# Attention scores of a window one step sooner, in the second halves of their PSUM banks

## The chip, the cores and the metric

The kernel runs on one core of a Trainium2 chip. The metric is the device time of one execution in microseconds (us); the time shown is the median of three runs. A core has five queues of instructions that run beside each other and wait for each other by semaphores: TensorE (PE in the profile), VectorE (DVE), ScalarE (ACT), GpSimd (POOL) and SyncE (SP), which here issues all DMAs.

## The reference

A network of two layers on 16 images of 128 channels by 56 by 56 pixels, in float32. The change lies in the first layer, a block with routed window attention. An image is cut into 7 by 7 = 49 windows of 8 by 8 pixels. For each window the four windows whose mean keys fit its mean query best are selected, and each of its 64 pixels attends, in 4 heads of 32 channels, to the 4 * 64 = 256 pixels of the selected windows:

```python
x = x + _dwconv(x, pos_w, pos_b)
y = _ln(xh, ln1_g, ln1_b)
qkv = y @ qkv_w + qkv_b
logits = jnp.einsum('bpc,bqc->bpq', q_win * SCALE, k_win)
_, idx = jax.lax.top_k(logits, TOPK)
kv_sel = jax.vmap(lambda t, i: t[i])(kv_pix, idx)
...
att = jnp.einsum('bpqhd,bpkhd->bphqk', q_pix * SCALE, k_sel)
att = jax.nn.softmax(att, axis=-1)
o = jnp.einsum('bphqk,bpkhd->bpqhd', att, v_sel)
...
o = (o + lepe) @ wo_w + wo_b          # lepe: 5x5 depthwise convolution of the values
xh = xh + o
z = gelu(_ln(xh) @ mlp_w1 + mlp_b1) @ mlp_w2 + mlp_b2
```

The second layer (a 3x3 convolution, a scan over sequences of 8 tokens and a group norm) isn't touched.

## The kernel before

`layer0` works on the images one after the other. For each there are 49 steps (`step(im, nxt, t)`, t is the window) and then the feed-forward part `mlp(im, nxt)`, which also ends the work on the last row of windows. Beside the attention of image `im`, the steps carry the first normalisation and projections of the next image `nxt`, the output projection and second normalisation of the row of windows before, the 5x5 convolution tap by tap on VectorE (`convolve_on`), and the 3x3 position convolution of later images on POOL (`beside_to`).

The order within each engine is the program's own: `_chain` ties every instruction to the one before it on its engine, so no scheduler moves anything. What waits for what between engines is found by the Tile framework from the tiles that instructions read and write. Buffers of a tile name turn over in pools of 1, 2, 3 or 6.

One window t passes through these stages:

- `gather` (L393): four DMAs on SP bring the selected windows' keys and values into `sel` (six buffers). Step t issues the gather of window t + 5; the first five are issued in the MLP of the image before. SP also loads an image's pixels in steps 20 and 24 (`load`, L288), and stores the results of the MLP.
- `scores` (L410): four matmuls of TensorE (eight instructions in the profile) write the scores of two heads into the first 256 columns of bank 0 of the PSUM tile `ps`, and of the other two into those of bank 1. `ps` has one buffer of two banks of 512 columns; the second halves stay unused.
- `largest` (L420): VectorE takes the maximum over the 256 scores, of both banks in one instruction, into the statistics tile `sst` (three buffers).
- `exponentials` (L424): ScalarE, once for each bank, with the negative maximum as bias and the sum as a second output, into the tiles `e` (three buffers).
- `inverse` (L432): VectorE takes the reciprocal of the sums; `weights` (L436): POOL multiplies.
- In step t + 1 TensorE transposes the weights into `ptt` and ScalarE copies them to `att`; in step t + 2 `attend` (L468) multiplies by the values. The values of `sel` are transposed into `pvt` for two windows at once (L446).

`open_step` is scores and maximum together. In step t they are those of window t; those of window 0 stand near the end of the MLP of the image before. The MLP's first hidden block (L549) uses bank 0 of `ps` too.

Of the kernel before, what the change touches and what calls it, by code (L numbers as in the profile page):

```python
# [12 lines left out]
AF = mybir.ActivationFunctionType  # L13
ALU = mybir.AluOpType
AX = mybir.AxisListType
# [6 lines left out]
NW = WIN * WIN  # L22
# [187 lines left out]
def layer0(ctx: ExitStack, tc: tile.TileContext, x, t, x1, conv):  # L210
# [11 lines left out]
    nc = tc.nc  # L222
# [35 lines left out]
    ps = banks.tile([P, 2, 512], F32, tag="ps", name="ps")  # L258


    bias = cst.tile([P, 6], F32, tag="bias", name="bias")
    for i in range(6):
        w, b = (wqkv[:, i, :], ln1_b) if i < 3 else (wm1[:, i - 3, :], ln2_b)
# [24 lines left out]
    def load(b, two):  # L288
        nc.sync.dma_start(pads[b % 2][64 * two : 64 * two + 64, 1 : H + 1, 1 : W + 1], xv[b, two])
# [33 lines left out]
    def squared(n):  # L323
        sq = held["sq"] = w1.tile([P, BLK], F32, tag="sq", name=f"sq_{n}")
        nc.scalar.activation(sq, held["pc"], AF.Square)
# [5 lines left out]
    def deviation(n):  # L331
        rstd = held["rstd"] = w1.tile([P, BLK], F32, tag="rstd", name=f"rstd_{n}")
        nc.scalar.activation(rstd, held["pv"], AF.Ln, bias=eps)
        nc.scalar.activation(rstd, rstd, AF.Exp, scale=-0.5)
# [3 lines left out]
    def windows(im, i):  # L338

        n = f"{im['b']}_{i}"  # L340
        y = held["y"] = w1.tile([P, BLK], F32, tag="y1", name=f"y1_{n}")
        nc.vector.tensor_mul(
            y.rearrange("c (w r x) -> c w r x", w=WIN, r=8),
            held["pc"].rearrange(by_row, r=8, w=WIN),
            held["rstd"].rearrange(by_row, r=8, w=WIN),
        )
        if i == 0:
            im["sum"] = w2.tile([P, NW], F32, tag="ysum", name=f"ysum_{n}")
            im["kv"] = w2.tile([P, NW, WP, 2], F32, tag="kv", name=f"kv_{n}")
        nc.vector.tensor_reduce(  # L350
            im["sum"][:, WIN * i : WIN * i + WIN], y.rearrange("c (w p) -> c w p", p=WP), AX.X, ALU.add
        )
# [5 lines left out]
    def keep(im, i, s):  # L358
        src = held["pq", s].rearrange("c (w p) -> c w p", p=WP)
        if s == 0:  # L360
            q = im["q"][i] = w1.tile([P, WIN, WP], F32, tag=f"q{i}", name=f"q_{im['b']}_{i}")
            nc.scalar.activation(q, src, AF.Identity, bias=bias[:, 0:1], scale=SCALE)
        else:
            kv = im["kv"][:, WIN * i : WIN * i + WIN, :, s - 1]
            nc.scalar.activation(kv, src, AF.Identity, bias=bias[:, s : s + 1])
# [27 lines left out]
    def gather(im, w):  # L393
        sel = im["sel", w] = w6.tile([P, TOPK, WP, 2], F32, tag="sel", name=f"sel_{im['b']}_{w}")
        if w % 2 == 0:
            n = min(2, NW - w)
            _, im["at"] = nc.values_load_multi_w_load_instructions(
                im["line"][:, w : w + n, :].rearrange("o w j -> o (w j)"), engines=(mybir.EngineType.SP,),
                min_val=0, max_val=NW - 1, skip_runtime_bounds_check_because="the indices are at most 48",
            )  # L400
        vs = im["at"][TOPK * (w % 2) :]
        for j in range(TOPK):
            nc.sync.dma_start(
                sel[:, j, :, :].rearrange("c p s -> c (p s)"),
                im["kv"][:, bass.ds(vs[j], 1), :, :].rearrange("c o p s -> c (o p s)"),
            )

    def scores(im, w):  # L410

        q, sel = im["q"][w // WIN][:, w % WIN, :], im["sel", w]
        for h in range(HEADS):
            p, s = divmod(h, 2)
            rows = slice(HD * h, HD * h + HD)
            nc.tensor.matmul(  # L416
                ps[64 * s : 64 * s + 64, p, 0:256], lhsT=q[rows], rhs=sel[rows, :, :, 0].rearrange("c j p -> c (j p)"), start=True, stop=True
            )

    def largest(im, w):  # L420
        st = im["st", w] = w3.tile([P, 3, 2], F32, tag="sst", name=f"sst_{im['b']}_{w}")
        nc.vector.tensor_reduce(st[:, 0, :], ps[:, :, 0:256], AX.X, ALU.max, negate=True)  # L422

    def exponentials(im, w):  # L424
        st = im["st", w]
        im["e", w] = [w3.tile([P, 256], F32, tag=f"e{p}", name=f"e{p}_{im['b']}_{w}") for p in range(2)]
        for p, e in enumerate(im["e", w]):
            nc.scalar.activation(  # L428
                e, ps[:, p, 0:256], AF.Exp, bias=st[:, 0, p : p + 1], accum_out=st[:, 1, p : p + 1]
            )  # L430

    def inverse(im, w):  # L432
# [35 lines left out]
    def attend(im, w):  # L468

        at, v = im["att", w], im["v", w]  # L470
        out = po[:, (w % WIN) * WP : (w % WIN + 1) * WP]
        for h in range(2):
            for head in range(HEADS):
                p, s = divmod(head, 2)
                rows = slice(HD * head, HD * head + HD)
                nc.tensor.matmul(
                    out[rows], lhsT=v[:, h, rows], rhs=at[:, p, h, s * WP : (s + 1) * WP],
                    start=(h == 0), stop=(h == 1), skip_group_check=True,
                )
# [41 lines left out]
    def collect(im, r):  # L521
        o = held["o"] = w1.tile([P, BLK], F32, tag="o", name=f"o_{im['b']}_{r}")
        nc.vector.tensor_add(
            o.rearrange("c (r w x) -> c r w x", r=8, w=WIN),
            po[:, 0:BLK].rearrange("c (w r x) -> c r w x", w=WIN, r=8),
            im["lepe", r].rearrange("c (r w x) -> c r w x", r=8, w=WIN),
        )
# [5 lines left out]
    def residual(im, r):  # L533
        xh = im["xh"][r]
        nc.vector.scalar_tensor_tensor(xh, held["pw"], wo_b, xh, ALU.add, ALU.add)

    def second(im, r):
        y2 = im["y2"][r] = w1.tile([P, BLK], F32, tag=f"y2{r}", name=f"y2_{im['b']}_{r}")
        nc.vector.tensor_mul(y2, held["pc"], held["rstd"])
# [49 lines left out]
    def open_step(im, t):  # L589
        scores(im, t)  # L590
        largest(im, t)

    def step(im, nxt, t):
        r, c = divmod(t, WIN)
        b = im["b"]
        n = f"{b}_{t}"
        out, row = (im, r - 1) if r else (images[b - 1], NBLK - 1)
        old, new = r > 0 or b > 0, nxt is not None
        if t + AHEAD < NW:
            gather(im, t + AHEAD)  # L600
        if t == 0 and early and not new:
            conv.load(0)
        if t in (20, 24) and b + 2 < NB:
            load(b + 2, t // 4 - 5)

        if c < 3 and new and r:
            keep(nxt, r - 1, c)
        if c == 2 and old:
            residual(out, row)
        if c == 3 and old:  # L610
            squared(n)
        if c == 4 and old:
            deviation(n)
        if c == 5 and new:
            squared(n)
        if c == 6 and new:
            deviation(n)
        if t > 0 or b == 0:
            open_step(im, t)
        if t > 1:  # L620
            attend(im, t - 2)
        if c == 1 and r:
            collect(im, r - 1)
        if c == 4 and old:
            second(out, row)
        if c == 6 and new:
            windows(nxt, r)
        convolve_on(TAPS[c] - 1)
        if new:
            if t == 1:  # L630
                position(nxt, 1, (8,))
            if t in ENDS:
                position(nxt, 2 + ENDS.index(t), (8,))
            if t < 45:
                beside_to(b + 1, LEAD + -(-(ROUND - LEAD) * (t + 1) // 45))
            else:
                beside_to(b + 2, 3 * (t - 44) // 2)
        exponentials(im, t)
        inverse(im, t)
        if t in (1, 8, 17, 27):  # L640
            surround(im, 3 + (1, 8, 17, 27).index(t))
        if t in (36, 44) and new:
            surround(nxt, (t - 36) // 8)
        weights(im, t)
        if c == 1 and new and r:
            project(g0, 2)
        waits = c in (1, 4, 6)
        if not waits:
            piece(im, nxt, out, row, c, r)
        if t > 0:  # L650
            transpose_weights(im, t - 1)
            keep_weights(im, t - 1)
        if c % 2 == 0:
            transpose_values(im, t)
            keep_values(im, t)
        convolve_on(1)
        if waits:
            piece(im, nxt, out, row, c, r)
# [83 lines left out]
    start = len(nc.cur_bb.bb.instructions)  # L742
    _act_set(tc, EXP_LN)
    im = images[0]
# [49 lines left out]
    for b in range(NB):  # L794
        im, nxt = images[b], images[b + 1] if b + 1 < NB else None
# [575 lines left out]
```

## Time and profile before

| | |
|---|---|
| median of three runs | 8305.27 us (8295.65 to 8312.71) |
| the profiled execution | 8300.8 us, its span 8299.0 us |
| mean granted clock of TensorE | 0.984 |
| TensorE, VectorE, ScalarE, POOL busy | 94%, 92%, 69%, 85% of the span |
| first layer | to about 3150 us of the span |
| one image in the first layer | about 188 us, of them 146 us from the scores of window 1 to those of window 48 |

How to read the profile's lines. A group's line gives source line, engine, operation, output <- inputs, shapes and count; then the busy time in us and the mean of one instruction in ns; then how long the engine was idle just before these instructions, and who ended most of that. A line of a timeline gives the start in us, the length, the engine and the operation; in square brackets how long the engine had been idle before, and for whom. `SPq` is SP's queue; for it the length covers all issues of the line, with the waits between them. PEld is the loading of weights into TensorE, which runs beside its matmuls.

### The profile page before, as it was taken

To read this page: it belongs to the slowest core of one execution; us is meant where nothing else is said; L and a number is where in the kernel's file an instruction comes from. 1 tells how busy PE (TensorE), PEld (TensorE's weight loads), DVE (VectorE), ACT (ScalarE), POOL (GpSimd) and SP (SyncE) were. 2 spreads that over 40 slices of the span, in tenths; PEclk is the share of its full clock that TensorE was granted. 3 is DMA by queue.
4 is the path that set the end of the run, shared out by engine and by line. 5 is a ranking of instruction groups with operands and counts; after the bars stand their busy time and mean duration, and the time that the engine had idled before them with its cause. 6 is when DMAs were issued, how large, how long until landed. Compare 5 with 4: busy or idle time off the path is not lost.

```text
span 8299.0 us, 151691 instructions
## 1 busy us (share of the span) xinstructions
PE 7837.1 (94%) x53308; PEld 3375.2 (41%) x53308; DVE 7631.6 (92%) x10124; ACT 5685.7 (69%) x10691; POOL 7030.7 (85%) x5584
## 2 busy tenths in 40 slices
PE   6999999999999998999999999999999999999998
PEld 3444444444444453333333333333333333333333
DVE  8999999999999976999999999999999999999998
ACT  4777777777777755666666666766666666666665
POOL 7888888888888725899989989999989989989997
PEclk8999999999999998999999999999999999999998
DMA  3333333333333223333333334334334334334333
GB/s 72 87 86 85 82 89 87 87 87 89 90 88 87 74 79 83 87 93 98 101 94 99 97 91 105 92 96 105 85 102 107 86 101 103 89 98 106 90 91 85
DMA packets 765478, 757.89 MB, mean 91 GB/s; under 512 B 189616, under 2 KB 664880, under 8 KB 762800
## 3 DMA queue, kind: packets, MB, share of 16 engines
q1 hardware_dynamic: 764720, 748.19, 35.3%
q8 instruction: 426, 6.98, 0.4%
q14 instruction: 332, 2.72, 0.1%
HBM read 439.61 MB, written 102.76 MB: 65 GB/s over the span
## 4 chain that ended last, share of the span: by engine, by line
PE 52%; DVE 21%; POOL 11%; ACT 10%; issue 5%; DMA 0%; SPq 0%; ACTq 0%; DVEq 0%; POOLq 0%
PE a L997 11%; PE pq L185 9%; PE pq L1043 6%; POOL xh L317 5%; PE x L1008 4%; DVE lepe L519 4%; PE pq L917 4%; DVE h L1015 3%; POOL tap L315 3%; PE pq L1077 3%; DVE sst L422 2%; PE pq L956 2%; PE pq L1049 2%; ACT e L428 2%; DVE a L1025 2%
## 5 line engine op out<-in xcount | busy, mean ns | idle before, releaser
L1034 POOL TENSOR_TENSOR cst<-h,cb 128x1792 f32<-128x1792 f32 x784 | 3129.5, 3998 | 342.6 <-DVE h L1030 273.1
L1000 ACT ACTIVATE a<-a 128x896 f32<-128x896 f32 x1568 | 1415.8, 903 | 1191.7 <-PE x L1008 961.0
L1015 DVE TENSOR_TENSOR h<-x,bb 128x896 f32<-128x896 f32 x1568 | 1698.2, 1083 | 134.1 <-PE x L1008 100.5
L519 DVE SCALAR_TENSOR_TENSOR lepe<-vpad,lep,lepe 128x448 f32<-128x448 f32 x2688 | 1717.8, 678 | 0.5
L1008 PE MATMUL x<-dtx,amask 32*128 32x448 f32 x6272 | 1620.9, 593 | 42.1 <-DVE h L1015 32.5
L997 PE MATMUL a<-dt,adec 32*128 32x448 f32 x6272 | 1616.3, 591 | 38.6 <-DVE h L1030 36.8
L1025 DVE TENSOR_TENSOR a<-a,h 128x896 f32<-128x896 f32 x1344 | 1466.1, 1091 | 69.3 <-ACT a L1000 64.9
L1030 DVE TENSOR_TENSOR h<-a,h 128x896 f32<-128x896 f32 x1344 | 1465.8, 1091 | 42.0
L438 POOL TENSOR_SCALAR e<-e,sst,zero 128x256 f32<-128x256 f32 x1568 | 855.3, 555 | 566.9 <-DVE sst L434 514.0
L428 ACT ACTIVATE e<-ps,sst 128x256 f32<-128x256 f32 x1568 | 727.0, 469 | 541.2 <-DVE sst L422 492.1
L997 PEld LDWEIGHTS a<-dt,adec 32*128 32x128 f32 x6272 | 472.8, 184 | 1037.9 <-issue 295.1
L317 POOL TENSOR_TENSOR xh<-xh,tap 128x448 f32<-128x448 f32 x749 | 859.4, 1147 | 33.9
L185 PE MATMUL pq<-pad,conv 128*128 128x448 f32 x1890 | 834.7, 559 | 0.0
L1043 PE MATMUL pq<-cst,sel 128*32 128x448 f32 x6272 | 731.3, 551 | 0.0
L422 DVE TENSOR_REDUCE sst<-ps 128x2 f32<-128x512 f32 x784 | 540.5, 689 | 99.6 <-PE ps L416 76.9
L146 ACT ACT_TABLE_LOAD x484 | 621.0, 1283 | 9.5 <-PEq L1362 0.7
L416 PE MATMUL ps<-sel,q 32*64 32x256 f32 x6272 | 541.1, 414 | 55.7 <-ACT e L428 45.9
L460 PE MATMUL ptt<-ident,e 128*128 128x128 f32 x3136 | 521.5, 282 | 73.4 <-POOL e L438 64.5
L1008 PEld LDWEIGHTS x<-dtx,amask 32*128 32x128 f32 x6272 | 473.7, 184 | 266.7 <-DVE h L1015 243.2
L460 PEld LDWEIGHTS ptt<-ident,e 128*128 128x128 f32 x3136 | 371.0, 142 | 373.4 <-issue 185.5
L466 ACT COPY att<-ptt 128x512 f32<-128x512 f32 x784 | 457.8, 584 | 64.8 <-PE ptt L460 54.9
L185 PEld LDWEIGHTS pq<-pad,conv 128*128 128x128 f32 x1890 | 324.2, 189 | 357.9 <-issue 350.2
(182 smaller groups left out, 12453.2 us busy)
## 6 DMA issues: line engine op xcount, KB each, us to landing
sel<-kv SPq DMA_DIRECT2D x3136, 64.0 KB
bb<-db SPq DMA_DIRECT2D x336, 448.0 KB
cb<-dc SPq DMA_DIRECT2D x336, 448.0 KB
x<-r SPq DMA_DIRECT2D x112, 224.0 KB
pad<-x SPq DMA_DIRECT2D x16, 1568.0 KB
db<-bs SPq DMA_DIRECT2D x112, 224.0 KB
dc<-cs SPq DMA_DIRECT2D x112, 224.0 KB
bb<-db SPq DMA_DIRECT2D x112, 224.0 KB
```

Source lines behind the costliest of these rows:

```text
L185: self.nc.tensor.matmul(bank[:, 0:BLK], lhsT=self.weights[:, k, :], rhs=self.pad[:, 8 * i + dy : 8 * i + dy + 8, dx : dx + W], start=(k == ...
L317: nc.gpsimd.tensor_add(im["xh"][i], im["xh"][i], held["tap"])
L428: nc.scalar.activation(e, ps[:, p, 0:256], AF.Exp, bias=st[:, 0, p : p + 1], accum_out=st[:, 1, p : p + 1])
L519: nc.vector.scalar_tensor_tensor(out, src, lep[:, k : k + 1], acc, ALU.mult, ALU.add)
L997: nc.tensor.matmul(a[:, k, :], lhsT=adec[rows, l4, :], rhs=p["dt"][rows, h, :], start=True, stop=True)
L1000: nc.scalar.activation(p["a", l, jp], p["a", l, jp], AF.Exp)
L1008: nc.tensor.matmul(x[:, k, :], lhsT=mask[rows, l4, :], rhs=p["dtx"][rows, h, :], start=True, stop=True)
L1015: nc.vector.tensor_mul(p["h", l][:, own(jp), :], px["x"], weight)
L1025: nc.vector.tensor_mul(a, a, before)
L1030: nc.vector.tensor_add(h, p["a", l, jp], h)
L1034: nc.gpsimd.tensor_mul(c, p["h", l], p["gate", 1, l].unsqueeze(1).to_broadcast([P, 4, BLK]))
L1043: nc.tensor.matmul(py[32 * j : 32 * j + 32], lhsT=sel[:, l4, :], rhs=p["c", l][:, j, :], start=False, stop=(l % 4 == 3), skip_group_check= ...
```

## The change

Scores, maximum and exponentials of odd windows use columns 256 to 511 of the two banks, those of even windows columns 0 to 255. Step t issues scores and maximum of window t + 1 in the place where those of window t stood. Step 0 of the first image issues those of window 0 as well; in later images these stay in the MLP. Step 48 issues none. Exponentials, reciprocal, weighting and all that comes later keep their steps.

```diff
+    def half(w):
+        return slice(256 * (w % 2), 256 * (w % 2) + 256)
+
     def scores(im, w):
...
             nc.tensor.matmul(
-                ps[64 * s : 64 * s + 64, p, 0:256], lhsT=q[rows], rhs=sel[rows, :, :, 0].rearrange("c j p -> c (j p)"), start=True, stop=True
+                ps[64 * s : 64 * s + 64, p, half(w)], lhsT=q[rows], rhs=sel[rows, :, :, 0].rearrange("c j p -> c (j p)"), start=True, stop=True
             )
 
     def largest(im, w):
...
-        nc.vector.tensor_reduce(st[:, 0, :], ps[:, :, 0:256], AX.X, ALU.max, negate=True)
+        nc.vector.tensor_reduce(st[:, 0, :], ps[:, :, half(w)], AX.X, ALU.max, negate=True)
 
     def exponentials(im, w):
...
             nc.scalar.activation(
-                e, ps[:, p, 0:256], AF.Exp, bias=st[:, 0, p : p + 1], accum_out=st[:, 1, p : p + 1]
+                e, ps[:, p, half(w)], AF.Exp, bias=st[:, 0, p : p + 1], accum_out=st[:, 1, p : p + 1]
             )
...
-        if t > 0 or b == 0:
+        if t == 0 and b == 0:
             open_step(im, t)
+        if t + 1 < NW:
+            open_step(im, t + 1)
         if t > 1:
             attend(im, t - 2)
```

## The prediction

> **What bounds the kernel now.** The change touches the attention steps of the first layer alone, so I read the page for the shares, then the view of the score tile `ps` (who waits for it), then the timeline of one image's start and of the SP queue.
>
> ```profile
> PE 7837.1 (94%) x53308; PEld 3375.2 (41%) x53308; DVE 7631.6 (92%) x10124; ACT 5685.7 (69%) x10691; POOL 7030.7 (85%) x5584
> L428 ACT ACTIVATE e<-ps,sst 128x256 f32<-128x256 f32 x1568 | 727.0, 469 | 541.2 <-DVE sst L422 492.1
> L422 DVE TENSOR_REDUCE sst<-ps 128x2 f32<-128x512 f32 x784 | 540.5, 689 | 99.6 <-PE ps L416 76.9
> L416 PE MATMUL ps<-sel,q 32*64 32x256 f32 x6272 | 541.1, 414 | 55.7 <-ACT e L428 45.9
> ```
>
> TensorE and VectorE are both full to over nine tenths. The 492.1 us that ScalarE waits for the maximum look like the prize, but ScalarE is 69% busy and costs nothing by waiting. What the engines that set the pace lose around the scores is small: TensorE 45.9 us before L416 until an exponential has left the banks; VectorE 76.9 us before the maximum, and (view of `ps`) 60.5 us before the reciprocal L434.
>
> The second resource is SP's queue, which isn't in the busy shares. Each step gathers one window's selection with four DMAs:
>
> ```profile
> 1244.73 62.54 SPq L403 DMA_DIRECT2D sel<-kv  x84
> 1307.37 0.68 SPq L289 DMA_DIRECT2D pad<-x  x1
> 1308.82 14.32 SPq L403 DMA_DIRECT2D sel<-kv  x16
> 1323.18 0.66 SPq L289 DMA_DIRECT2D pad<-x  x1
> 1324.60 60.81 SPq L403 DMA_DIRECT2D sel<-kv  x76
> ```
>
> ```profile
> 1724.17 0.68 PE L416 MATMUL ps<-sel,q 32*64 32x256 f32 x8 [0.53 <-DMA sel<-kv]
> ...
> 590.69 0.36 PE L446 MATMUL pvt<-ident,sel 128*128 128x128 f32 x1 [0.53 <-DMA sel<-kv]
> ```
>
> 84 issues in 62.54 us are 2.98 us for a gather, waits included; a step takes 3.06 us (scores at 1261.50 and, seven steps on, 1282.91). SP is nearly full. The two image loads in steps 20 and 24 (L289) throw it back: the 16 issues between them took 14.32 us, 3.58 a gather. After them SP can't catch up. The second fence, from the timelines of two other images, shows TensorE already waiting for a gather, in scores and in transposes.
>
> How near it is follows from the trace's records of each gather's landing (updates of its semaphore), set against the starts of the scores. In the image that begins at 1432 us:
>
> ```
> window  last issue ends  landed   scores of it   scores one step sooner
> 24      1495.23          1496.55  1504.66        1501.83
> 30      1520.08          1523.87  1524.01        1520.39
> 33      1529.55          1532.28  1533.45        1529.48
> 48      1575.65          1578.64  1578.86        1576.25
> ```
>
> Up to window 25 a selection lies there 5 to 8 us before it is wanted even one step sooner. From 26 on it comes about when the step before takes its scores, or after. At window 30 it landed 0.14 us ahead of its use, and 3.48 us behind the place that the scores are to be moved to.
>
> **The change part by part.** (1) Other halves. Same matmuls, reduction and exponentials, same sizes; no row changes. Cost nil.
>
> (2) In step t TensorE now does scores t+1, VectorE maximum t+1, both in the places where those of t stood; steps 1 to 47 keep the order of all engines but for the index. What ScalarE waits for decides. The exponentials of t follow maximum t+1 in program order and read the same two banks. In the changed program as built, the wait of e(t) on VectorE's semaphore is for the count that maximum t+1 gives (in the old one, maximum t), and the scores of t+1 still wait for e(t-1). So the halves are not treated as separate: in every step scores, maximum and exponentials follow each other in the same places. The row for what that chain costs is 45.9 us (L416 on ACT e). By addresses alone, e(t) needs only its own maximum, a step old, and up to 45.9 us would go. The Trainium skill (PSUM — Partial Sum Buffer, section on bank collisions) says that two engines on one bank and the same partitions collide even at different columns, so guard by bank and not by address; by that rule the gain is 0. No run here shows a collision, but the built wait is the rule's. I take 0. The 492.1 us wait stays, as do the 60.5 and 76.9.
>
> (3) Start of an image. Before, maximum 0 stands in the MLP, and step 0 has neither scores nor maximum:
>
> ```profile
> 1242.92 0.68 DVE L422 TENSOR_REDUCE sst<-ps 128x2 f32<-128x512 f32 x1
> 1243.52 0.67 DVE L557 SCALAR_TENSOR_TENSOR r<-po,vec,xh 128x448 f32<-128x448 f32 x1
> 1243.69 0.47 ACT L428 ACTIVATE e<-ps,sst 128x256 f32<-128x256 f32 x1 [4.11 <-DVE sst L422]
> 1244.11 1.86 DVE L519 SCALAR_TENSOR_TENSOR lepe<-vpad,lep,lepe 128x448 f32<-128x448 f32 x3
> ...
> 1245.88 0.15 DVE L434 RECIPROCAL sst<-sst 128x2 f32<-128x2 f32 x1
> ...
> 1246.75 0.98 PE L460 MATMUL ptt<-ident,e 128*128 128x128 f32 x4 [1.30 <-POOL e L438]
> ```
>
> Now scores 1 come first; they wait for maximum 0 (ends 1243.60) and start at about 1243.72. Maximum 1 can start 0.82 us after (as at 1274.10 and 1274.92, where it waited), 1244.54, instead of the taps at 1244.19: 0.35 us of wait and 0.69 of work. Exponential 0 slips to 1245.3 to 1246.2, which the three taps (1.77) cover. Reciprocal 0 goes from 1245.88 to 1246.95; POOL, idle there, weights 1.07 later; TensorE, idle for POOL, transposes 1.07 later; after that it has no gap to make it good, and maximum and scores of the next steps follow. So about 1.07 us later per image. In step 48 scores and maximum are gone (0.68 and 0.69 us), but nothing gains: TensorE then waits for weights 47 on POOL (1202.31 to 1203.40), VectorE for ScalarE's deviation (ends at 1203.65). 15 images by 1.07 are 16.0; for image 0, which issues both in step 0, 1.0. Sum 17; ends 8 (half of it caught up) and 22.
>
> (4) Gathers. SP's order is unchanged, so no gather is issued sooner, but scores t+1 want theirs one step sooner. Once TensorE has waited, everything is later by that, while SP, itself the late one, goes on; so an image pays its worst shortfall once. Worst margins (start of the scores one step sooner, minus landing) of images 0 to 15, us: -2.14, 0.18, -3.20, -1.50, -0.98, -3.48, -0.29, -3.48, -3.20, -1.63, -3.23, -2.33, 0.15, -1.19, 3.58, -2.20. The negatives add up to 28.9; 0.14 each from landing to start makes 30.7. Off it: about 0.35 per image for gaps in the engines that close while TensorE stands (maximum starts up to 0.4 after it could), 13 by 0.35 or 4.6; and in the four or five images where SP is late from the start, the 1.07 of (3) is time for SP too, 4. Remains 22. Queued behind the waiting scores are TensorE's eight attend matmuls, projections and transposes; VectorE's maximum waits for them, and all taps behind it. Ends: 10 (gaps absorb more), 36 (nothing absorbed, a worse draw of landings).
>
> (5) What else moves past what. The statistics tile has three buffers: maximum t+1 now waits in step t for POOL's weighting of t-2 instead of t-3. In the trace the shortest time from the end of weights t-2 to the maximum in step t is 1.82 us, so no wait; if POOL fell behind by that, VectorE would pay the rest. Selections that were freed by their scores are freed up to one step sooner; SP is bound by its issues more than by buffers, so I take 0; it might give back a few us (inside the low end of (4)). ScalarE's and POOL's orders don't change.
>
> Sum: 0 + 17 + 22 = +39 us. The profiled execution's own time is 8300.8 (span 8299.0); the median shown is 8305.3, 4.5 above. On the median: 8344.
>
> **Rivals.**
> A. Slower as summed, 8344; chance 0.66.
> B. Slower by more: no absorption, larger lateness because a shifted image meets other transfers: 22 and 36, +58, 8363; 0.22. For it: worst margins vary from 0.2 to -3.5 between images with the same code. Against: most images agree with each other in the late steps to about 1 us.
> C. Hidden: half of (3) caught up and gaps absorb the gathers, 8 and 5: +13, 8318; 0.08. For it: TensorE idles 6%. Against: those idles lie behind ScalarE and POOL, which a late gather makes late too.
> D. Faster: the exponentials run a step ahead after all. Then TensorE's 45.9 us before L416 go; gathers still cost 22: -24, 8281. It decides as soon as more than half of those 45.9 are won. Against it: the wait in the built program; for it, only the addresses. 0.04.
> That the change doesn't do what it says is part of A: scores do come sooner, but nothing is let go earlier.
>
> **Numbers.** A measurement of this kernel can tell about 0.2% (16.6 us) from no change. 8344 is A's. The range 8322 to 8369 takes in A with its ends and most of B. Faster 0.04 (D), same 0.07 (most of C), slower 0.89.
>
> **Right or wrong in the next profile.** Right: ScalarE's wait before the exponentials still near 490 us and put down to the maximum; waits of TensorE before the scores put down to `sel<-kv` of some 20 to 30 us where the view of `ps` now has 9.1; steps 1 to 25 and the second layer as long as now; the first transposes of an image a us later. Wrong: the exponentials' wait falls to a few us (D), or no new DMA waits before the scores (C).

## The result and the profile after

The changed kernel takes 8348.0 us (median of six runs, 8338.15 to 8350.69), the kernel before 8303.64 us on the same chip (six runs, 8295.65 to 8312.71). The ratio is 1.0052, interval 1.0041 to 1.0063: slower by 44.4 us. The prediction was 8344. The profiled execution has a span of 8346.8 us and a granted clock of 0.982 (before: 8299.0 and 0.984).

Three groups on the page of the changed kernel answer to those shown of before. L431, L425 and L419 are the exponentials, maximum and scores, three lines further down in the file:

```profile
PE 7855.6 (94%) x53308; PEld 3377.9 (40%) x53308; DVE 7633.1 (91%) x10124; ACT 5687.4 (68%) x10691; POOL 7042.9 (84%) x5584
L431 ACT ACTIVATE e<-ps,sst 128x256 f32<-128x256 f32 x1568 | 728.2, 469 | 582.2 <-DVE sst L425 566.5
L425 DVE TENSOR_REDUCE sst<-ps 128x2 f32<-128x512 f32 x784 | 540.1, 689 | 119.6 <-PE ps L419 92.0
L419 PE MATMUL ps<-sel,q 32*64 32x256 f32 x6272 | 543.4, 415 | 96.9 <-ACT e L431 41.2
```

Counts and means are those of before (469, 689 and 415 ns; the last was 414). The idle times have grown. The wait that the change might have abolished, ScalarE's for the maximum, has gone from 492.1 to 566.5 us. TensorE's wait for an exponential to leave the banks is still there, 41.2 us where it was 45.9. Both exponentials of a window still wait for a maximum, and the scores still wait for the exponentials.

The view of the tile `ps` says who is late now. The first two lines are from its part on what ended the idle time (us, times), the others from the part on who waited:

```profile
  DVE sst L425: 613.2, 610
...
  DMA sel<-kv: 28.0, 13
...
  ACT e L431: 566.5, 592
...
  DVE sst L425: 92.0, 167
  DVE sst L437: 61.1, 123
  PE ps L419: 60.4, 117
```

The gathers ended 9.1 us of waits before the scores, in two places; now 28.0 us, in 13. Of these, 8.5 and 8.9 us are the wait for the very first gather of the program, which the change doesn't touch; so 0.5 us in one place became 19.1 us in twelve. SP's queue in the image that starts at 1257 us shows why. Lengths cover all issues of a line with the waits between them:

```profile
1262.70 63.65 SPq L403 DMA_DIRECT2D sel<-kv  x84
1326.44 0.68 SPq L289 DMA_DIRECT2D pad<-x  x1
1327.89 13.94 SPq L403 DMA_DIRECT2D sel<-kv  x16
1341.87 0.66 SPq L289 DMA_DIRECT2D pad<-x  x1
1343.30 56.98 SPq L403 DMA_DIRECT2D sel<-kv  x70
```

It is the same queue as before, with the same two loads and 13.94 us for the four gathers between them (before 14.32). SP delivers no sooner; only the user has come closer. What that looks like when it happens is in the timeline of the next image:

```profile
1538.61 1.13 PE L419 MATMUL ps<-sel,q 32*64 32x256 f32 x8
1539.88 0.69 DVE L425 TENSOR_REDUCE sst<-ps 128x2 f32<-128x512 f32 x1 [1.21 <-PE ps L419]
1540.60 0.47 ACT L431 ACTIVATE e<-ps,sst 128x256 f32<-128x256 f32 x1 [1.25 <-DVE sst L425]
...
1543.28 0.68 PE L419 MATMUL ps<-sel,q 32*64 32x256 f32 x8 [1.09 <-DMA sel<-kv]
1544.08 0.69 DVE L425 TENSOR_REDUCE sst<-ps 128x2 f32<-128x512 f32 x1 [1.08 <-PE ps L419]
1544.81 0.48 ACT L431 ACTIVATE e<-ps,sst 128x256 f32<-128x256 f32 x1 [1.43 <-DVE sst L425]
```

The scores at 1543.28 are those of window 30. Its gather landed at 1543.14, and TensorE, VectorE and ScalarE all stand until then: 1.09, 1.08 and 1.43 us of idle time, one behind the other. By the records of landings, in 13 of the 16 images scores start right upon the landing of their gather (0.14 us after it), most often those of window 30.

To place the loss, the span is cut at the starts of the transposes `ptt` of each image (windows 0, 25 and 48) and summed over the images. "Between images" is from the last transposes of an image to the first of the next, 15 times. Sums in us, from the traces; kernels are named by the experiments below. Each row is one execution, which lies up to 7 us from its kernel's median:

| kernel | to first ptt | windows 0 to 25 | windows 25 to 48 | between images | rest (second layer) |
|---|---|---|---|---|---|
| before | 119.2 | 1257.2 | 1145.3 | 585.9 | 5191.5 |
| changed | 118.3 | 1257.3 | 1176.5 | 597.5 | 5197.2 |
| e1 other halves only | 118.8 | 1255.9 | 1150.6 | 587.3 | 5186.5 |
| e2 sooner only | 118.4 | 1258.8 | 1174.0 | 596.3 | 5194.9 |
| e3 six gathers in the MLP | 119.3 | 1257.1 | 1148.3 | 690.8 | 5190.5 |
| e4 the same, old order | 119.0 | 1265.9 | 1141.0 | 675.2 | 5186.6 |
| e5 sixth gather in step 0 | 119.9 | 1259.0 | 1176.9 | 596.1 | 5192.1 |
| e6 scores 1 later in step 0 | 117.5 | 1258.7 | 1177.9 | 597.2 | 5193.2 |
| e7 no loads | 117.7 | 1261.9 | 1143.7 | 596.1 | 5189.9 |
| e8 exponentials sooner too | 117.8 | 1269.6 | 1162.1 | 603.0 | 5196.6 |
| e9 six gathers, spread | 119.1 | 1256.0 | 1152.7 | 592.7 | 5187.9 |
| e10 the same, old order | 118.0 | 1259.4 | 1141.7 | 583.4 | 5181.6 |
| e11 e9, scores 1 at the end of step 0 | 117.7 | 1253.4 | 1151.6 | 602.0 | 5194.9 |
| e12 loads on ScalarE's queue | 148.9 | 1279.7 | 1143.5 | 596.3 | 5191.4 |

Before to changed: windows 25 to 48 grow by 31.2 us, the stretches between images by 11.6, windows 0 to 25 by 0.1. The rest grows by 5.7, which is noise: the second layer is the same in all 14 kernels, and its stretch lies anywhere from 5181.6 to 5197.2. Of the 31.2 us, 27.7 arise in windows 25 to 30. The 0.1 hides two things that nearly cancel: windows 0 to 25 of the last image, where the tightest gather is that of window 6, grow by 2.8 us (88.2 to 91.0), and four other images are about 1.1 us shorter there because TensorE's clock wasn't halved (see the last section).

### The profile page after: what moved, and what is told of

It reads as the page before. It is cut to its first block, busy times and chain, and to the rows that moved or that the text cites. A ratio compares the mean times of both kernels' runs of the same rounds, so it can differ in the third digit from the quotient of the medians.

```text
span 8346.8 us, 151676 instructions
## 1 busy us (share of the span) xinstructions
PE 7855.6 (94%) x53308; PEld 3377.9 (40%) x53308; DVE 7633.1 (91%) x10124; ACT 5687.4 (68%) x10691; POOL 7042.9 (84%) x5584
## 4 chain that ended last, share of the span: by engine, by line
PE 55%; DVE 20%; ACT 10%; POOL 8%; issue 5%; DMA 1%; SPq 1%; ACTq 0%; DVEq 0%; POOLq 0%
PE a L1002 11%; PE pq L185 9%; PE pq L1048 6%; PE x L1013 4%; DVE lepe L522 4%; PE pq L922 4%; DVE h L1020 3%; POOL xh L317 3%; POOL e L441 3%; PE pq L1082 2%; PE pq L961 2%; DVE sst L425 2%; DVE a L1030 2%; PE pq L1054 2%; ACT e L431 2%
## 5 line engine op out<-in xcount | busy, mean ns | idle before, releaser
L431 ACT ACTIVATE e<-ps,sst 128x256 f32<-128x256 f32 x1568 | 728.2, 469 | 582.2 <-DVE sst L425 566.5
L425 DVE TENSOR_REDUCE sst<-ps 128x2 f32<-128x512 f32 x784 | 540.1, 689 | 119.6 <-PE ps L419 92.0
L419 PE MATMUL ps<-sel,q 32*64 32x256 f32 x6272 | 543.4, 415 | 96.9 <-ACT e L431 41.2
```

## The experiments

The theory: all of the loss is gathers that are late for scores one step sooner (behind the two loads), and the maximum that step 0 gained; the other halves do nothing, since scores, maximum and exponentials exclude each other by bank. The main rival at first was that the halves or the sixth use of a buffer cost something by themselves. All edits are against the changed kernel unless "old order" is said. Medians are of this experiment's runs, and ratios are against the kernel before on the same chip (8300.7 to 8302.24 us).

**e1: other halves only.** The old place of scores and maximum, the new columns.

```diff
-        if t == 0 and b == 0:
+        if t > 0 or b == 0:
             open_step(im, t)
-        if t + 1 < NW:
-            open_step(im, t + 1)
```

> Only the first part of the change: odd windows use the second halves of the banks, scores and maximum stay in their own step. My theory (the halves cost and bring nothing; both losses come from issuing a step sooner): no difference from before, 8304 us give or take 8. Rival (a bank written and read in both halves costs something by itself, or frees something): some of the 44 us of the change, up or down, shows here, 8320 us or more.

8302.09 us, ratio 1.0004 (0.9995 to 1.0013). From the new columns alone no difference is measured.

**e2: sooner only.** All windows in columns 0 to 255, order of the change. `half` alone is edited:

```diff
-        return slice(256 * (w % 2), 256 * (w % 2) + 256)
+        return slice(0, 256)
```

> The order of the changed kernel, but all windows in the first halves; what is computed changes, since the exponentials of a window then read the scores of the next. My theory (the framework guards by bank, so every wait is the same with and without the second halves): the time of the changed kernel, 8348 us give or take 8, and ScalarE's wait for the maximum near 570 us as there. Rival (the second halves do let something run earlier, and the loss would be greater without them): above 8360 us.

8342.44 us, ratio 1.0050 (1.0036 to 1.0064), the changed kernel's within the intervals. The view of `ps`, who waited:

```profile
  ACT e L431: 563.5, 591
...
  PE ps L419: 59.4, 119
```

With one half per bank ScalarE waits 563.5 us, with two 566.5, and TensorE 59.4 and 60.4. If the second half had freed anybody, e2 would have longer waits than the changed kernel. So what remains of the change, with or without halves, is an order that is one step earlier for scores and maximum, with the exponentials chained to it as tightly as before.

**e3 and e4: more lead.** Gathers six windows ahead instead of five, in the changed kernel (e3) and in the old order (e4). The room for it comes from the output tile, which goes from three buffers to two.

```diff
-    AHEAD = 5
+    AHEAD = 6
...
-        r = w3.tile([P, BLK], F32, tag="r", name=f"r_{im['b']}_{i}")
+        r = w2.tile([P, BLK], F32, tag="r", name=f"r_{im['b']}_{i}")
```

> The changed kernel with gathers issued six windows ahead instead of five (seven buffers of the selection; the MLP's output tile has two buffers instead of three to make room). My theory (31 us of the 44 are scores that wait for late gathers in steps 26 to 48): these waits go, steps 25 to 48 of an image take what they took before (some 71 us), and 10 to 15 us are left from the starts of the images: 8314 to 8320 us. Rival (the late steps are longer because TensorE and VectorE work in a worse order there): stays above 8340 us.

> The control to the one above: the kernel before, with gathers six windows ahead and two buffers of the MLP's output tile. My theory: TensorE waits for gathers only 9 us there, so 8295 to 8305 us. Rival (a deeper lead helps in any order, or two buffers cost): outside 8290 to 8310 us.

8407.85 us (1.0130, 1.0114 to 1.0145) and 8393.25 us (1.0112, 1.0097 to 1.0128): both far slower than expected. The time went elsewhere. The list of waits from 300 to 2900 us of e3 has one new line; after the names come us in total, times and the longest:

```profile
DVE r L560 <- DMA x<-r: 110.8, 14, 8.9
```

SP's queue of e4 in the MLP shows the reason:

```profile
472.55 17.01 SPq L403 DMA_DIRECT2D sel<-kv  x24
489.66 13.43 SPq L558 DMA_DIRECT2D x<-r  x6
```

All gathers issued ahead stand in one block in the MLP. The stores of the MLP stand behind it for 17 us, and with two output buffers VectorE waits for a store (16.3 us in the changed kernel, 110.8 here). That cost, some 93 us, has nothing to do with the question; the stretch that it doesn't reach answers it. Windows 25 to 48 are back at 1148.3 us in e3, near the 1145.3 of the kernel before (e4, the old order with the same gathers, has 1141.0). And with the old cause gone on both sides, the change costs 14.6 us (e3 less e4) where it cost 44.4. One step more lead, one step of lead used: the greater part of that term is the gathers.

**e5: the sixth gather without that side effect.** Three output buffers again; the room comes from putting the tile `o` into the buffer of the squares. The MLP issues five gathers as before, and step 0 issues a second one.

```diff
-    AHEAD = 5
+    AHEAD = 6
...
-        o = held["o"] = w1.tile([P, BLK], F32, tag="o", name=f"o_{im['b']}_{r}")
+        o = held["o"] = w1.tile([P, BLK], F32, tag="sq", name=f"o_{im['b']}_{r}")
...
+        if t == 0 and b:
+            gather(im, AHEAD - 1)
...
-                for w in range(AHEAD):
+                for w in range(AHEAD - 1):
```

> The changed kernel with gathers six windows ahead, again, but with the MLP's output tile left at three buffers (room comes from two tiles that share a buffer) and the sixth gather issued in step 0 instead of in the MLP. My theory: the 93 us that both kernels with six gathers in the MLP lost were stores waiting in SP's queue, and go; steps 25 to 48 add up to about 1148 us over the images as with the gathers before (changed kernel 1177, before 1145); what is left of the change is its image starts, 8312 to 8322 us. Rival (a sixth buffer in flight costs in itself): above 8340 us.

8351.63 us, ratio 1.0066 (1.0052 to 1.0080): no gain. The buffer is there, but not the gather:

```profile
1262.26 65.81 SPq L403 DMA_DIRECT2D sel<-kv  x88
1328.17 0.68 SPq L289 DMA_DIRECT2D pad<-x  x1
1329.04 16.12 SPq L403 DMA_DIRECT2D sel<-kv  x16
```

SP now issues 22 gathers before the load instead of 21, but starts on the image no sooner, and 65.81 us for 22 are 2.99 us each, about the pace of a step (3.06). Windows 25 to 48 stay at 1176.9. This queue, whose limit is its issues, gained nothing by a place to put them. The expectation failed on a point that the prediction had itself made (SP is nearly full). From it the second theory: the lead has to be won where SP is idle, in the MLP.

**e6: scores 1 later within step 0.** In step 0, they and their maximum come behind the exponentials of window 0, ahead of the reciprocal.

```diff
-        if t + 1 < NW:
+        if 0 < t and t + 1 < NW:
             open_step(im, t + 1)
...
         exponentials(im, t)
+        if t == 0:
+            open_step(im, 1)
         inverse(im, t)
```

> The changed kernel, but in step 0 scores and maximum of window 1 stand behind the exponentials of window 0 instead of ahead of them; all later steps as changed. My theory (ahead of them they hold up the first exponentials, reciprocal, weights and transposes of an image): the MLP part, from the last transposes of an image to the first of the next, returns from 39.6 us to 38.9 us each; 10 us less in all, 8333 to 8342 us, if the transposes come sooner and what follows keeps up. Rival (the moved work is just paid a few instructions later): 8345 us or more.

8339.31 us, ratio 1.0041 (1.0028 to 1.0055). The median lies in the range of the theory, but the interval doesn't tell it from the changed kernel, and the trace (of the slowest of its five executions, 8346.32 us) has 597.2 us between images as against 597.5: the gain that was expected there isn't to be seen. The maximum is still ahead of the reciprocal, so its length is paid in either place.

**e7: no loads.** The image loads of steps 20 and 24 are left out; everything else is the changed kernel.

```diff
-        if t in (20, 24) and b + 2 < NB:
-            load(b + 2, t // 4 - 5)
```

> The changed kernel without the two loads of a later image in steps 20 and 24; the images after the second are therefore computed from old pixels. My theory (these loads throw SP's queue back, and the gathers behind them are what TensorE waits for): the waits in steps 26 to 48 go nearly all, 8313 to 8322 us. Rival (gathers are late for SP's own pace, loads or not): above 8335 us.

8318.36 us, ratio 1.0021 (1.0012 to 1.0030): 29.6 us less than the changed kernel. Windows 25 to 48 take 1143.7 us, those between images 596.1. The two losses come apart: without loads the first is gone whole, the second untouched. SP's queue of e7 in the same image:

```profile
1247.49 136.70 SPq L403 DMA_DIRECT2D sel<-kv  x176
```

44 gathers without a break, 3.11 us each, about the pace of the steps. SP then follows the consumers, where in the changed kernel they follow SP.

**e8: exponentials one step sooner as well,** so that a whole step lies between them and the reciprocal, with the gathers of e5.

```diff
-        exponentials(im, t)
-        inverse(im, t)
+        if t + 1 < NW:
+            exponentials(im, t + 1)
```

with the exponentials of window 0 and the reciprocal of each step moved to the step's start.

> The whole chain one step sooner: the exponentials of window t + 1 stand in step t too, behind its maximum, and the reciprocal of window t at the start of step t; gathers six windows ahead as in the kernel beside it. Scores still wait for the exponentials before them, as in every version. My theory: scores, maximum and exponentials follow each other as before, so that chain gives nothing; but the reciprocal finds its sums ready (VectorE waits 61 us for them now) and POOL's weights come up to 2 us sooner than the transposes need them (TensorE waits some 70 us for POOL): 8270 to 8300 us. Rival (these waits were hidden behind other limits, TensorE being full): 8310 us or more.

8350.85 us, ratio 1.0057 (1.0044 to 1.0071). In images where no gather is late the steps are no shorter (70.7 us for windows 25 to 48; 70.8 in e7 and e9, which have the order of the change), windows 0 to 25 are 12 us longer than in the changed kernel and the stretches between images 5.5. Against e5, whose gathers it has, windows 25 to 48 are 14.8 us shorter and the others longer by more. From the list of waits from 300 to 2900 us:

```profile
DVE sst L425 <- PE ps L419: 114.3, 126, 5.3
PE ps L419 <- DMA sel<-kv: 21.2, 19, 4.9
```

The maximum's wait for the scores doubles (57.3 us in the changed kernel, same window). The time is the rival's. Its reason, that TensorE (busy for 94%) is the limit of these steps, fits but isn't shown apart.

**e9 and e10: the sixth gather where SP is idle.** The buffers of e5, and the gathers of the MLP issued one in each of its blocks, between its stores; in the order of the change (e9) and in the old one (e10).

```diff
-            if m == 2 and nxt:
-                for w in range(AHEAD):
+            if m >= 2 and nxt:
+                for w in range(m - 2, AHEAD if m == count else m - 1):
```

> The changed kernel with gathers six windows ahead (seven buffers, the MLP's output tile keeps three, two other tiles share a buffer), those of the first six windows spread over the blocks of the MLP, one window a block, so that SP has them issued before step 0 and no store waits behind many of them. My theory (late gathers are 30 of the 44 us, and SP gets ahead only where it is idle, in the MLP): the scores' waits for gathers go, steps 25 to 48 add up to about 1148 us, and 8312 to 8322 us remain. Rival (SP is behind again from the first loads on, whatever its lead): above 8335 us.

> The same six gathers, spread over the MLP, in the kernel before. My theory: its 9 us of waits for gathers and some of the 16 us that VectorE waits for stores in the MLP go, 8280 to 8297 us, and it stays 15 us or more ahead of the changed kernel with the same gathers. Rival (those waits are hidden): 8300 us or more.

e9: 8315.94 us, ratio 1.0018 (1.0009 to 1.0027). e10: 8292.91 us, ratio 0.9992 (0.9983 to 1.0001). SP's queue of e9 in the MLP before the image at 1257 us:

```profile
1225.77 3.86 SPq L403 DMA_DIRECT2D sel<-kv  x4
1229.72 0.54 SPq L561 DMA_DIRECT2D x<-r  x1
1230.45 2.43 SPq L403 DMA_DIRECT2D sel<-kv  x4
```

Gathers and stores alternate, and no store waits for more than one gather. In the list of waits from 300 to 2900 us the gathers fall from 18.0 us in the changed kernel to 5.7:

```profile
PE ps L419 <- DMA sel<-kv: 5.7, 8, 1.6
```

So 32 of the 44 us are won back by placing prefetches alone. The old order is still faster by 23.0 us with the same gathers: 11.0 in windows 25 to 48, 9.3 between images, the rest in stretches that vary from run to run. So not all that remains lies at the starts: e9 still has those 5.7 us of waits, and in three of its images, but in none of e10, the clock was halved for 3.4 us in windows 25 to 48. e10 has the lowest median of all, but its interval still holds 1; that it beats the kernel before isn't shown.

**e11: e9 with scores 1 at the very end of step 0,** behind all else of the step.

```diff
-        if t + 1 < NW:
+        if 0 < t and t + 1 < NW:
             open_step(im, t + 1)
...
+        if t == 0:
+            open_step(im, 1)
```

> As the first of these (changed, six gathers spread over the MLP), with scores and maximum of window 1 at the very end of step 0, behind the reciprocal of window 0, where the kernel before has them but for a few instructions. My theory (the starts lose the length of the maximum, 0.69 us, which stands ahead of the first reciprocal; step 48 gives nothing back): the MLP part returns to 38.9 us an image, and about half of the rest is paid in step 1, whose own scores and maximum follow at once: 4 to 8 us below the first of these. Rival (the loss at the starts is only moved): within 3 us of it.

8314.97 us, ratio 1.0018 (1.0009 to 1.0027), within 1 us of e9. Between images there are 602.0 us instead of 592.7, in windows 0 to 25 there are 1253.4 instead of 1256.0. The time is that of the rival, that the loss only moves. But the stretch that was to become shorter, that between images, became longer by 9.3 us; why stays open.

**e12: the loads off SP.** They are issued by ScalarE's queue.

```diff
-        nc.sync.dma_start(pads[b % 2][64 * two : 64 * two + 64, 1 : H + 1, 1 : W + 1], xv[b, two])
+        nc.scalar.dma_start(pads[b % 2][64 * two : 64 * two + 64, 1 : H + 1, 1 : W + 1], xv[b, two])
```

> The changed kernel with the image loads of steps 20 and 24 issued by ScalarE instead of SP; the gathers stay on SP and five windows ahead. My theory has two parts of what a load costs SP: its own issue with the pause around it, about 1.4 us, which goes; and the later wait of a gather until a load eight DMAs before it has landed, about 2.3 us, since the DMAs share eight semaphores in turn, which stays. So a third to a half of the 30 us: 8328 to 8340 us. Rival 1 (the issue alone is what counts): 8318 to 8325 us. Rival 2 (it is the traffic on the DMA engines): 8345 us or more.

8362.52 us, ratio 1.0075 (1.0061 to 1.0089). Part of the reason was not thought of: the two loads of image 1 now stand behind ScalarE's work on image 0 and are issued at 91.6 us, not at 16.3, so that the first transposes come 30.6 us later. Without these it would be about 8332 us, in the range of the theory. Windows 25 to 48 take 1143.5 us, as in e7, but that isn't a gain of this size: the loss has moved across the cut. Windows 20 to 25 take 271.3 us in e12, 247.0 in the changed kernel and 246.9 in that of before. From window 0 to 48 e12 takes 2423.2 us, the changed kernel 2433.8, e7 2405.6, the kernel before 2402.5: about a third of the loss is won back, as the theory had it. The timeline around one load and the list of waits from 300 to 2900 us show a piece of what is lost in exchange:

```profile
2123.38 0.63 ACTq L289 DMA_DIRECT2D pad<-x  x1
2124.06 0.54 ACT L325 ACTIVATE sq<-g 128x448 f32<-128x448 f32 x1 [2.28 <-DMA sel<-kv]
ACT sq L325 <- DMA sel<-kv: 14.6, 9, 2.8
```

Before a load ScalarE waits for the landing of an earlier gather whose semaphore the load is to use, 14.6 us in nine places. And the traffic can be felt: gathers 24, 25, 28 and 29 land 4.7 to 6.4 us after their last issue (medians), where they took 1.3 to 1.4 in the changed kernel. So e7 shows that the loads make the gathers late; how much of it is their place in SP's queue and how much their traffic e12 doesn't separate.

## Why the prediction was right

**Other halves (0) and the chain (0).** Right. e1 measures nothing for the halves, and e2 the whole change without them. The rule weighed there (the Trainium skill, PSUM — Partial Sum Buffer, section on bank collisions: engines on one bank and the same partitions collide at any columns) agrees with the traces in what was built: the guard doesn't go by columns, and the 41.2 us in front of L419 are still there. Whether it goes by bank or by the whole tile `ps` can't be told here, as the scores wait for both exponentials at once. That unguarded accesses would collide isn't shown by any run here, since the guard was in all of them.

**The start of an image (+17).** Right in kind, too large: 11.6 us between images, and nothing at image 0. The timeline of the image that begins at 1257 us:

```profile
1260.89 0.68 DVE L425 TENSOR_REDUCE sst<-ps 128x2 f32<-128x512 f32 x1
...
1261.62 0.68 PE L419 MATMUL ps<-sel,q 32*64 32x256 f32 x8 [0.89 <-DVE sst L425]
...
1262.37 0.69 DVE L425 TENSOR_REDUCE sst<-ps 128x2 f32<-128x512 f32 x1 [0.21 <-PE ps L419]
...
1264.75 0.16 DVE L437 RECIPROCAL sst<-sst 128x2 f32<-128x2 f32 x1
```

Scores 1 do wait for maximum 0, and maximum 1 comes ahead of the taps. From maximum 0 to reciprocal 0 it is 3.86 us where it was 2.96, 0.90 more. The sum had 0.35 of wait and 0.69 of work; the wait is 0.21. (The 0.35 was reckoned from taps at 1244.19; by the line shown they started at 1244.11.) Of the 1.07 an image expected, 11.6 / 15 = 0.77 came. This image isn't the usual one: in eleven of the 15 starts maximum 1 doesn't wait at all, and nine starts grow by 0.64 to 0.67 us, near the 0.69 of the maximum alone. The other six changed by -0.7 to 1.9 us; in four of these the clock was halved for 1.6 to 2.9 us more in the changed kernel's trace. So the wait of 0.35 was the mis-sized part, and the work was right. The other half of the step held: step 48 gives nothing back, as the place of its maximum is idle time now, the next instruction waiting for ScalarE (the last figure in brackets):

```profile
1221.48 0.63 DVE L342 TENSOR_TENSOR y<-g,rstd 128x448 f32<-128x448 f32 x1 [0.88 <-ACT rstd L334]
```

e6 and e11 agree: whichever place in step 0 the additional work has, it is paid.

**Late gathers (+22).** The mechanism was right: one jump per image, at its worst window. In the image before the one at 1257 us, for instance, the transposes keep their distance to those of the kernel before until window 27; at window 28, the transposes just behind scores 30, it grows by 3.4 us, at the next by 0.6, and stays.

That the sum of the worst margins, 30.7 us, is nearly what was measured (31.2) is in part luck, for the 31.2 are not all gathers. TensorE's waits for gathers in these steps grew from 2.4 us (0.5 before scores, the rest before transposes) to 19.1, by 16.7. Most of the remainder goes with a term that the prediction had at nothing: the granted clock. The records of the clock show a stretch of 3.4 us at half clock in windows 25 to 48 of ten of the first 15 images, in the kernel before in two. What one costs can be read from e7, where no gather is late: its two images with such a stretch take 72.2 and 72.3 us, the other thirteen 70.8. Eight more at 1.5 us make an estimate of 12 us.

In five of the ten the stretch begins 0.4 to 1.3 us after the start of the scores that waited for their gather, as in the image above, and the image takes 70.8 us, its wait and about 1.4 us more:

```profile
1160.67 0.68 PE L419 MATMUL ps<-sel,q 32*64 32x256 f32 x8 [2.62 <-DMA sel<-kv]
...
1157.90:1161.30 3.40, 0.78 (x14) 0.26 (x12) 1.17 (x3) 1.33 (x3) 2.87 (x4) 1.00 0.40 98
1161.30:1164.70 3.40, 3.40 (x26) 2.30 (x24) 2.53 (x5) 1.06 (x5) 1.18 (x3) 0.51 0.37 106
```

(The last two lines give a stretch, its us, busy time of PE, PEld, DVE, ACT and POOL with counts, granted clock, DMA share and GB/s.) In the other five it comes some 6 us ahead of scores 30 or without any late gather. The last image but one is of these: it had 3.6 us to spare, waited for no gather, and lost 1.9 us. Nine kernels whose gathers are mostly in time have such stretches in none to three images, and four of the five whose gathers are late (changed, e2, e5, e6) in seven to eleven; e8, with 21.2 us of waits, has them in one. So late gathers seem to bring them on, but that isn't shown.

The two subtractions, 4.6 us for gaps that close and 4 us for what SP gains by the late start, can't be judged, since the waits alone stayed below the 22. The last image, whose worst window is 6, lost nothing in these steps and 2.8 us before them.

**Statistics buffers (0).** No run shows a wait of the maximum for POOL on account of them.

So the total is close through errors that partly cancel, and in the greatest term through a part that wasn't in the working. Against the 39 of the sum the starts gave 6 less (11.6 and nothing at image 0), the late steps 9 more, and the second layer some 6 of noise: 48, the difference of the two spans (47.8). The medians differ by 44.4.

## What to carry to other kernels

Moving a consumer one step sooner takes a step from the lead of every producer that isn't moved with it: compare landing times with the new place, and the pace of the queue's issues (here 2.98 of 3.06 us per step) with the step. A queue that is full by its issues wasn't helped here by a buffer more (e5); prefetches in one block where it is idle won the late steps but held up the stores (e3), and in small pieces between the stores they did no harm (e9). Two halves of a PSUM bank are not two buffers as long as the guard doesn't go by columns, and work moved from the end of a loop to its start costs its length if the hole at the end can't be filled. Before a sum of waits is taken for the cause of a loss, look at the granted clock of the same stretch.

## What the runs showed of the hardware

TensorE's granted clock drops to half for some microseconds at the start of most images, and not of all. The view by stretches of the changed kernel for the image at 1257 us:

```profile
1263.60:1266.60 3.00, 2.11 (x12) 1.03 (x13) 3.00 (x7) 1.16 (x6) 1.59 (x3) 0.52 0.32 92
1266.60:1269.60 3.00, 3.00 (x24) 0.95 (x26) 2.19 (x6) 1.39 (x5) 3.00 (x7) 0.50 0.31 90
```

and for one some 950 us later, with the same instructions:

```profile
2216.30:2219.30 3.00, 1.75 (x21) 0.97 (x20) 2.87 (x6) 1.38 (x5) 2.27 (x3) 1.00 0.38 136
2219.30:2222.30 3.00, 2.18 (x18) 0.88 (x14) 3.00 (x8) 1.47 (x6) 2.52 (x4) 1.00 0.30 87
```

At half clock TensorE is full for three microseconds where it would have had room. Of the images between the first and the last, the four that escaped take 77.0 us for windows 0 to 25, the others about 78.1. So some 1.1 us of an image go with the clock, more than the 0.66 us that a start lost by the change. What decides whether an image escapes isn't shown. It also happens within an image, as the explanation above has it, and not only behind a wait. In the timeline of the late gather further up, the scores at 1538.61 took 1.13 us and those at 1543.28 took 0.68; the view by stretches has:

```profile
1537.00:1539.00 2.00, 2.00 (x7) 0.62 (x10) 1.67 (x4) 1.32 (x5) 1.67 (x5) 0.50 1.40 141
```

That stretch of half clock lies ahead of the wait for the gather, not behind it.

An image load delays the gathers behind it in SP's queue twice. In the changed kernel the first issue behind a load takes 2.8 us (median), where others take 0.5, so that the four issues of gathers 26 and 30 take 4.8 and 4.6 us instead of 2.4. And these two land 3.0 and 3.7 us after their last issue, the others 1.35. Behind two loads, window 30 is the tightest. Why the first issue takes so long isn't shown. SP's DMAs use eight semaphores in turn, but at that issue the DMA eight places earlier had landed more than 3 us before, so it isn't the turn that holds it up. For e12's loads the turn counts: that is what ScalarE waits for there.
